# Gated delta-rule block: the decays take beta and the key norm as logarithms, and ScalarE takes over the roots

## The chip, the cores and the metric

The kernel runs on one core of one Trainium2 chip. The metric is the device time of one execution in microseconds. A NeuronCore has five instruction queues that run side by side and wait for one another through semaphores: TensorE (PE in the profile, with its weight loads as PEld), VectorE (DVE), ScalarE (ACT), GpSimd (POOL) and SyncE (SP), which here only issues DMAs. [...]

## What is computed

One transformer block in float32: an attention that supplies the hidden states, a gated delta rule over chunks of 64 tokens, and two feed-forward parts. The change touches only the delta rule. Cut to what matters:

```python
q = _l2norm(q); k = _l2norm(k)            # x * rsqrt(sum(x * x) + 1e-6)
beta = sigmoid(h @ W_b)
g = cumsum(-exp(A_log) * softplus(h @ W_a + dt_bias))     # in each chunk of 64
decay = tril(exp(g[:, None] - g[None, :]))
A = tril(-(k * beta) @ k.T * decay, -1)
T = inverse(I - A)
u = T @ (v * beta)
w = T @ (k * beta * exp(g))
...
core = core * rsqrt(mean(core * core) + 1e-6) * norm_w
core = core * silu(z)
return core @ W_out
```

There are 16 batches of 128 tokens (two chunks each), 16 key heads and 32 value heads of width 128.

## The kernel before

Attention comes first, in 32 blocks, and the delta rule starts while it is still running. The delta rule is cut into 64 **units**, each one key head (two value heads) with a group of four batches, that is 8 pairs of batch and value head. A loop over slots `n` runs the units as a software pipeline: in slot n the keys of unit n are made (`keys`), the key products of unit n-1 (`decays`), the values of unit n-7 (`values`), the outputs of unit n-8 (`outputs`), and unit n-10 is transposed and multiplied with its rows of `W_out` (`finish_unit`). In every four slots a batch of four units is inverted (`inverse`): 32 small triangular systems side by side, almost all on DVE, in a first and a second half that lie in two successive slots. `mergers` puts the 32x32 inverses together to 128x128 on PE.

Each step has a planned time between 0 and 24 in its slot, written by hand in the loop at the end. The steps of a slot are emitted in that order; the framework may then move an instruction a little, and each engine keeps the order that results. All PSUM tiles of this stage except `ps_out` come from one pool of six buffers, taken in turn: a tile waits for the one that was allocated six places earlier.

What the change touches:

- `logs` (lines 310 to 334): beta as 1 / (1 + exp(-x)), with an addition and a reciprocal on DVE (L323, L324), and the gates.
- `running` (336 to 347): cumulative sums of the gates by matmul. The rows go to DRAM (`sums`), the columns to SBUF (`off`).
- `load_sums` (428): for a **pair** of units, the sums of each broadcast over all partitions, 512 KB each, into a tile `aT` of 2048 columns.
- `fades` (436): for a pair, POOL subtracts `off` (L443) and masks (L444), and ACT takes one exponential of both (L448).
- `factors` (497), the last step of `keys`: POOL makes from the squared norms `nn` (L500, L502), by powers `kn` (L505: the norm and its inverse square), and the product `c` of beta and 1/norm² (L507).
- `weight` (519), the first step of `decays`: POOL multiplies the decays with `c` (L522). The products then multiply them with k kᵀ and k qᵀ on DVE (L534), which frees `ps_kq`. `diagonal` (537) writes the diagonal blocks to the tile that the inverse reads.
- `norm` (772), the last step of `outputs`: POOL adds the epsilon term (L775), takes the power -1/2 (L776) and multiplies z (L777).

Beside these, prediction and change speak of `conv` (459: one copy on ACT, three multiply-adds on DVE, L466), `row`, `times`, `merge8`, `products16` and `sums16` of the inverse (L568 to L628), `val_turn` (720: transposes of the values, `ps_vt`), `gate` (736: `ps_z` and its silu), `new_values` (748: `ps_y` and its copy to y) and `attend` (758: `ps_ot`).

ACT needs another set of function tables for Silu than for Exp and Ln; where the function changes, the build puts a table load (ACT_TABLE_LOAD) in front of it.

Of the kernel before, what the change touches and what calls it, by code (L numbers as in the profile page):

```python
# [15 lines left out]
P = 128  # L16
# [40 lines left out]
def tile_adaln_attn_ffn(  # L57
# [36 lines left out]
    powers = filled([P, 2, GS], 0.5, "powers")  # L94
    G.memset(powers[:, 1, :], -1.0)
    inv_root = filled([P, NP], -0.5, "inv_root")
# [38 lines left out]
    beta = keep.tile([P, NK, NB, 2], F32, name="beta")  # L135
# [14 lines left out]
    def attention():  # L150
# [144 lines left out]
        def output(g):  # L295
# [14 lines left out]
            def logs():  # L310
                if g > 1:
                    nc.sync.dma_start(out=h_dram[g], in_=hTs[g])
                ps = ps_b.tile([P, GS, 2 * NV], F32, name="ps_ba", tag="b")
                for j in range(GS):
                    for c in range(ND):
                        T.matmul(ps[:, j, :], lhsT=hTs[g][:, c, j * S : (j + 1) * S], rhs=wba[:, c, :],
                                 start=c == 0, stop=c == ND - 1)
                a = p1.tile([P, GS, NV], F32, name="a", tag="ga", bufs=1)
                e = p1.tile([P, GS, NV], F32, name="ea", tag="ge", bufs=1)

                A.activation(e, ps[:, :, 0:NV], AF.Exp, scale=-1.0)
                V.tensor_tensor(a, ps[:, :, NV:], dtb[:, None, :].to_broadcast([P, GS, NV]), ALU.add)
                V.tensor_scalar(e, e, 1.0, None, ALU.add)  # L323
                V.reciprocal(beta[:, :, g * GS : (g + 1) * GS, :].rearrange("p k b h -> p b k h"),  # L324
                             e.rearrange("p b (k h) -> p b k h", h=2))

                V.scalar_tensor_tensor(out=e, in0=a, scalar=-1.0, in1=a, op0=ALU.mult, op1=ALU.max)
                A.activation(e, e, AF.Exp, scale=-1.0)
                A.activation(e, e, AF.Ln, bias=one)
                V.scalar_tensor_tensor(out=a, in0=a, scalar=0.0, in1=e, op0=ALU.max, op1=ALU.add)  # L330
                gd = d["gd"] = p1.tile([P, NK, GS, 2], F32, name="gd", tag="gd", bufs=1)
                V.tensor_tensor(gd.rearrange("p k b h -> p b k h"), a.rearrange("p b (k h) -> p b k h", h=2),
                                nega.rearrange("p (k h) -> p k h", h=2)[:, None, :, :].to_broadcast([P, GS, NK, 2]),
                                ALU.mult)

            def running():
# [91 lines left out]
    def load_sums(n):  # L428

        t = sum_of[n] = pc.tile([P, 2, NP, S], F32, name="aT", tag="aT", bufs=5)  # L430
        for i in range(2):
            kh, g = units[n + i]
            nc.sync.dma_start(out=t[:, i].rearrange("p q t -> p (q t)"),
                              in_=sums[g][kh * NP : (kh + 1) * NP].rearrange("q t -> (q t)").partition_broadcast(P))

    def fades(n):

        def log(i):
            t = sum_of[n]
            kh, g = units[n + i]  # L440
            o = off[:, kh, g * GS : (g + 1) * GS].rearrange("p s h i -> p (s h) i")
            t4 = t[:, i].rearrange("p q (i c) -> p q i c", i=2)
            G.tensor_tensor(t4, t4, o[:, :, :, None].to_broadcast([P, NP, 2, C]), ALU.subtract)  # L443
            G.affine_select(out=t[:, i], in_=t[:, i], pattern=[[0, NP], [1, S]], compare_op=ALU.is_ge,  # L444
                            fill=-1e30, base=0, channel_multiplier=-1)

        def exp():
            A.activation(sum_of[n], sum_of[n], AF.Exp)  # L448

        return [lambda: log(0), lambda: log(1), exp]  # L450
# [20 lines left out]
    def keys(u):  # L471
# [10 lines left out]
        def silu(j):  # L482
            A.activation(d["kq"][:, :, j, :], d["kc", j], AF.Silu)  # L483
# [13 lines left out]
        def factors():  # L497
            tr = d["tr"][:, :, 0].rearrange("p (s j) -> p j s", j=2)
            nn = d["nn"] = pc.tile([P, 2, GS], F32, name="nn", tag="nn", bufs=10)
            G.tensor_scalar(nn[:, 0, :], tr[:, 0, :], 1e-6, None, ALU.add)  # L500

            G.tensor_scalar(nn[:, 1, :], tr[:, 1, :], 1e-6, P * P * 1e-6, ALU.add, ALU.mult)  # L502

            kn = d["kn"] = pc.tile([P, 2, GS], F32, name="kn", tag="kn", bufs=9)
            G.tensor_tensor(kn, nn[:, 0:1, :].to_broadcast([P, 2, GS]), powers, ALU.pow)  # L505
            d["c"] = pc.tile([P, GS, 2], F32, name="c", tag="c", bufs=2)
# [3 lines left out]
        return [lambda: qk(0), lambda: qk(1), lambda: silu(0), lambda: silu(1), square, norms, factors]  # L510

    def decays(u):
# [5 lines left out]

        def weight():
            n = index[u]  # L520
            dec = d["aT"] = sum_of[n - n % 2][:, n % 2]
            G.tensor_tensor(dec, dec, d["c"].rearrange("p s h -> p (s h)")[:, :, None].to_broadcast([P, NP, S]),  # L522
                            ALU.mult)
            d["bT"] = pc.tile([P, NP, S], F32, name="bT", tag="bT", bufs=7)
# [20 lines left out]
        return [weight, lambda: products(0), lambda: products(1), diagonal]  # L545
# [161 lines left out]
    def values(u):  # L707
# [9 lines left out]
        def silu(h):  # L717
            A.activation(d["vT", h], d["vT", h], AF.Silu)

        def val_turn(n):  # L720
# [4 lines left out]
            for j in range(2):  # L725
                s = 2 * n + j
                A.activation(d["v"][:, s, :, :], ps[:, j, :, :], AF.Copy, scale=d["kn"][:, 0, s : s + 1])
# [3 lines left out]
    def outputs(u):  # L731
# [4 lines left out]
        def gate(n):  # L736
# [8 lines left out]
            A.activation(d["z"][:, 4 * n : 4 * n + 4, :].rearrange("p q f -> p (q f)"),  # L745
                         ps.rearrange("p s f -> p (s f)"), AF.Silu)
# [25 lines left out]
        def norm():  # L772

            r = d["r"].rearrange("p (s h) -> p s h", h=2)
            G.tensor_tensor(r, r, d["nn"][:, 1, :][:, :, None].to_broadcast([P, GS, 2]), ALU.add)  # L775
            G.tensor_tensor(d["r"], d["r"], inv_root, ALU.pow)  # L776
# [3 lines left out]
                lambda: attend(0), lambda: attend(1), norm]  # L780
# [72 lines left out]
    for n in range(N + LAST):  # L853
# [14 lines left out]
        if n == 0:  # L868
            plan([lambda: load_sums(0)], [5])
# [278 lines left out]
```

## Time and profile before

| | us |
|---|---|
| three runs | 2427.54, 2430.64, 2430.76 (median 2430.64) |
| the profiled execution | 2431.28 |
| its span, from the first to the last instruction | 2429.6 |

| engine | busy us | share | instructions |
|---|---|---|---|
| PE | 2200.7 | 91% | 16248 |
| PEld | 1450.2 | 60% | 16248 |
| DVE | 1548.1 | 64% | 2102 |
| ACT | 1361.7 | 56% | 3008 |
| POOL | 1145.9 | 47% | 833 |

The profile comes from one execution with the hardware profiler. Busy shares are means over stages that have different limits: up to about 330 us attention and the first units run together, from there to about 1900 us the full pipeline, then it drains, and from about 2106 us the feed-forward parts run. The groups of instructions that the change removes or alters (count, busy us, mean ns of one):

| line, engine | what | count | busy | mean |
|---|---|---|---|---|
| L443 POOL | decays minus `off`, 128x1024 | 64 | 123.4 | 1929 |
| L444 POOL | causal mask, 128x1024 | 64 | 71.8 | 1124 |
| L500, L502 POOL | `nn`, 128x4 | 64 each | 15.6, 12.7 | 244, 198 |
| L505 POOL | `kn`, power, 128x8 | 64 | 106.9 | 1671 |
| L507 POOL | `c`, 128x8 | 64 | 51.8 | 810 |
| L522 POOL | weight, 128x1024 | 64 | 122.3 | 1911 |
| L775 POOL | r plus epsilon term, 128x8 | 64 | 30.8 | 481 |
| L776 POOL | power -1/2, 128x8 | 64 | 105.0 | 1640 |
| L777 POOL | z times r, 128x1024 | 64 | 132.2 | 2066 |
| L448 ACT | exponential of two units, 128x2048 | 32 | 61.2 | 1913 |
| all, ACT | table loads | 79 | 101.4 | 1283 |

Between two successive instructions of an engine there can be a wait; the trace names the instruction of another engine whose signal came last. A wait on PE costs time in the full pipeline, since PE is the engine with the least slack there; a wait on POOL as a rule costs none.

### The profile page before, as it was taken

How to read it: one execution, taken by the hardware profiler on the slowest of the kernel's cores; microseconds unless marked ns; L12 is line 12 of the kernel's file. 1: busy time of each engine (PE TensorE's matmuls, PEld its weight loads, DVE VectorE, ACT ScalarE, POOL GpSimd, SP SyncE). 2: the span in 40 equal slices, each digit the busy share in tenths (PEclk: the TensorE clock that was granted, in tenths of full speed). 3: DMA queues.
4: the chain of work that ended last, by engine and by line, in shares of the span. 5: the costliest groups of instructions: out<-in, count | busy, mean ns of one | idle time of the engine just before them, and what ended most of it. 6: DMA issues, size and time to landing. Idle time of an engine off the chain costs nothing. (4 is left out here: it accounts for less than half of the span.)

```text
span 2429.6 us, 41939 instructions
## 1 busy us (share of the span) xinstructions
PE 2200.7 (91%) x16248; PEld 1450.2 (60%) x16248; DVE 1548.1 (64%) x2102; ACT 1361.7 (56%) x3008; POOL 1145.9 (47%) x833
## 2 busy tenths in 40 slices
PE   7868759989999998989999998989999898999999
PEld 3433336766667666766666666766677686344445
DVE  4657878687776968687777868687876831311111
ACT  3566536766666666766666666766666574111110
POOL 4585535465555656465555656465556413700000
PEclk9889879999999999999999999999999999999999
DMA  1200022222222322322223222222322323000000
GB/s 56 91 17 15 24 56 76 70 66 71 68 66 77 104 72 64 75 68 68 68 80 86 82 73 64 77 66 68 85 69 80 89 52 123 26 0 20 9 0 18
DMA packets 289910, 148.37 MB, mean 61 GB/s; under 512 B 184241, under 2 KB 278193, under 8 KB 289713
## 3 DMA queue, kind: packets, MB, share of 16 engines
q1 hardware_dynamic: 287792, 141.44, 21.1%
q0 software_dynamic: 1344, 4.20, 0.5%
q8 instruction: 131, 2.15, 0.4%
q14 instruction: 67, 0.54, 0.1%
q10 hardware_dynamic: 576, 0.05, 0.0%
HBM read 119.13 MB, written 5.51 MB: 51 GB/s over the span
## 5 line engine op out<-in xcount | busy, mean ns | idle before, releaser
L466 DVE SCALAR_TENSOR_TENSOR cv<-ps_in,cw,cv 128x500 f32<-128x500 f32 (+2 forms) x768 | 540.2, 735 | 88.8 <-ACT cv L464 84.2
L455 PE MATMUL ps_in<-hT,w_v 128*128 128x512 f32 x512 | 281.5, 679 | 6.8 <-DVE z L770 4.6
L464 ACT ACTIVATE cv<-ps_in,cw 128x512 f32<-128x512 f32 x256 | 174.5, 682 | 182.7 <-PE ps_in L455 182.0
L770 DVE TENSOR_TENSOR z<-ps_ot,z 128x512 f32<-128x512 f32 x128 | 87.9, 687 | 289.9 <-ACT sq L768 289.9
L455 PE MATMUL ps_in<-hT,w_qk 128*128 128x512 f32 x512 | 251.3, 613 | 7.1 <-DVE z L770 6.2
L743 PE MATMUL ps_z<-w_gate,hT 128*128 128x256 f32 x1024 | 242.3, 379 | 1.7 <-DVE z L770 1.7
L800 PE MATMUL ps_out<-wo_head,zT 128*128 128x256 f32 x1024 | 238.8, 386 | 1.0 <-ACT zT L792 1.0
L500 POOL TENSOR_SCALAR nn<-turned 128x4 f32<-128x4 f32 x64 | 15.6, 244 | 419.4 <-DVE turned L495 316.8
L800 PEld LDWEIGHTS ps_out<-wo_head,zT 128*128 128x128 f32 x1024 | 189.0, 190 | 38.0 <-issue 10.7
L743 PEld LDWEIGHTS ps_z<-w_gate,hT 128*128 128x128 f32 x1024 | 189.4, 190 | 27.7 <-DVE z L770 2.6
L455 PEld LDWEIGHTS ps_in<-hT,w_v 128*128 128x128 f32 x512 | 104.6, 217 | 113.3 <-issue 105.2
L768 ACT ACTIVATE sq<-ps_ot 128x128 f32<-128x128 f32 x512 | 143.2, 280 | 31.6 <-PE ps_ot L762 23.0
L483 ACT ACTIVATE kq<-cv 128x512 f32<-128x512 f32 x128 | 80.1, 626 | 126.8 <-DVE cv L466 126.7
L756 ACT COPY y<-ps_y 128x512 f32<-128x512 f32 x128 | 75.0, 586 | 135.3 <-PE ps_y L755 130.6
L530 PEld LDWEIGHTS ps_kq<-kq 128*128 128x128 f32 x512 | 102.5, 203 | 73.4 <-issue 53.4
L455 PEld LDWEIGHTS ps_in<-hT,w_qk 128*128 128x128 f32 x512 | 94.2, 195 | 84.8 <-issue 67.0
L1055 POOL TENSOR_TENSOR o<-o,x_in 128x512 f32<-128x512 f32 x8 | 10.1, 1265 | 283.4 <-DVE o L1054 283.4
L777 POOL TENSOR_TENSOR z<-z,r 128x1024 f32<-128x1024 f32 x64 | 132.2, 2066 | 23.2 <-DVE z L770 20.4
L790 PE MATMUL ps_zt<-ident,z 128*128 128x128 f32 x512 | 88.9, 301 | 59.4 <-DVE aT L534 57.4
L530 PE MATMUL ps_kq<-kq 128*128 128x256 f32 x512 | 136.8, 391 | 0.0
L762 PE MATMUL ps_ot<-y,aT 128*128 128x128 f32 x1024 | 135.3, 275 | 0.0
L755 PEld LDWEIGHTS ps_y<-v,W 128*128 128x128 f32 x1024 | 123.3, 194 | 16.6 <-ACT W L701 10.8
(212 smaller groups left out, 5004.2 us busy)
## 6 DMA issues: line engine op xcount, KB each, us to landing
aT<-sums SPq DMA_DIRECT2D x64, 512.0 KB, 5.8
w_qk<-in_w_qkv_dram SPq DMA_DIRECT2D x128, 128.0 KB, 2.2
w_v<-in_w_qkv_dram SPq DMA_DIRECT2D x64, 256.0 KB, 2.7
w_gate<-in_w_z_dram SPq DMA_DIRECT2D x64, 256.0 KB, 2.7
wo_head<-in_w_out_dram SPq DMA_DIRECT2D x64, 256.0 KB, 2.7
diag<-bT SPq DMA_DIRECT2D x256, 32.0 KB, 2.0
W<-Uc SPq DMA_DIRECT2D x256, 32.0 KB, 2.0
T<-Tc SPq DMA_DIRECT2D x128, 32.0 KB, 1.9
```

What stands on the lines that cost most here:

```text
L455: T.matmul(ps, lhsT=w[:, c, blk, :], rhs=hTs[g][:, c, :], start=c == 0, stop=c == ND - 1)
L464: A.activation(cv, psv, AF.Copy, scale=cw[:, col, 3:4])
L466: V.scalar_tensor_tensor(out=cv[:, :, sh:], in0=psv[:, :, : S - sh], scalar=cw[:, col, 3 - sh : 4 - sh], in1=cv[:, :, sh:], op0=ALU.mult, ...
L530: T.matmul(ps[:, j, :, :], lhsT=d["kq"][:, s, 0, :], rhs=d["kq"][:, s, :, :], start=True, stop=True)
L743: T.matmul(ps[:, j, :], lhsT=hTs[g][:, c, t0 : t0 + S], rhs=w_gate[u][:, c, :], start=c == 0, stop=c == ND - 1)
L755: T.matmul(ps[:, j, :], lhsT=d["W"][:, p, :], rhs=v[:, p, :], start=True, stop=True)
L762: T.matmul(ps[:, j, :], lhsT=d["aT"][:, p, :], rhs=d["y"][:, p, :], start=True, stop=True)
L768: A.activation(sq, ps[:, j, :], AF.Square, accum_out=d["r"][:, p : p + 1])
L770: V.tensor_tensor(z, ps, z, ALU.mult)
L777: G.tensor_tensor(d["z"], d["z"], d["r"][:, :, None].to_broadcast([P, NP, S]), ALU.mult)
L790: T.transpose(ps[:, j, :], d["z"][:, 4 * n + j, :], ident)
L800: T.matmul(ps[:, j, :], lhsT=d["zT", n][:, 2 * j + h, :], rhs=w_o[u][:, h, :], start=kh == j == h == 0, stop=kh == NK - 1 and j == h == 1)
```

## The change

Beta and the key norm no longer enter as factors. The exponent of the decays gets their logarithms: `off` holds the cumulative gate plus softplus(-x), which is -log(beta), and a small tile `lk` = log(norm² + epsilon) is added for each unit before the subtraction. One exponential then gives decay, beta and 1/norm² together, so `weight` goes. `kn` = exp(lk / 2) serves the values, and the output norm is exp(-log(r) / 2). Both powers leave POOL. The load and five ACT instructions form one block per unit (`logarithms`): a load of the table set with Exp and Ln, the exponential of the unit before (128x1024), Ln and Exp of `r` of a unit nine slots back, Ln and Exp of the new key norms. By ordering edges the block stands behind every silu of the delta rule emitted before it and ahead of every later one (`silu_of`, `follow`). Decays are handled one unit at a time. Most planned times move; the `decays` products go from 4.5 and 9 to 18 and 21, the inverse's first half starts at 8, and the norm product comes one slot later.

```diff
-    powers = filled([P, 2, GS], 0.5, "powers")
-    G.memset(powers[:, 1, :], -1.0)
-    inv_root = filled([P, NP], -0.5, "inv_root")
+    small = filled([P, 1], 1e-6, "small")
...
-                A.activation(e, ps[:, :, 0:NV], AF.Exp, scale=-1.0)
+                sp = d["sp"] = p1.tile([P, GS, NV], F32, name="sp", tag="gs", bufs=1)
+                A.activation(sp, ps[:, :, 0:NV], AF.Exp, scale=-1.0)
...
-                V.tensor_scalar(e, e, 1.0, None, ALU.add)
-                V.reciprocal(beta[:, :, g * GS : (g + 1) * GS, :].rearrange("p k b h -> p b k h"),
-                             e.rearrange("p b (k h) -> p b k h", h=2))
+                A.activation(sp, sp, AF.Ln, bias=one)
...
-                    V.tensor_copy(off[:, :, g * GS : (g + 1) * GS, :, i].rearrange("p k b h -> p k (b h)"),
-                                  ps[:, 1 + i, :].rearrange("p (k q) -> p k q", k=NK))
+                    V.tensor_tensor(off[:, :, g * GS : (g + 1) * GS, :, i],
+                                    ps[:, 1 + i, :].rearrange("p (k b h) -> p k b h", k=NK, h=2),
+                                    d["sp"].rearrange("p b (k h) -> p k b h", h=2), ALU.add)
...
+        t = sum_of[n] = pc.tile([P, NP, S], F32, name="aT", tag="aT", bufs=9)
...
         def factors():
...
-            G.tensor_scalar(nn[:, 0, :], tr[:, 0, :], 1e-6, None, ALU.add)
-            G.tensor_tensor(kn, nn[:, 0:1, :].to_broadcast([P, 2, GS]), powers, ALU.pow)
-            G.tensor_tensor(d["c"], beta[:, kh, g * GS : (g + 1) * GS, :],
-                            kn[:, 1, :][:, :, None].to_broadcast([P, GS, 2]), ALU.mult)
+            G.tensor_scalar(nn, tr[:, 1, :], 1e-6, P * P * 1e-6, ALU.add, ALU.mult)
+        def fade():
+            t = d["aT"] = sum_of[index[u]]
+            o = pc.tile([P, GS, 2, 2], F32, name="o", tag="o")
+            G.tensor_tensor(o.rearrange("p s h i -> p s (h i)"),
+                            off[:, kh, g * GS : (g + 1) * GS].rearrange("p s h i -> p s (h i)"),
+                            d["lk"][:, :, None].to_broadcast([P, GS, 4]), ALU.add)
+            t4 = t.rearrange("p q (i c) -> p q i c", i=2)
+            G.tensor_tensor(t4, t4, o.rearrange("p s h i -> p (s h) i")[:, :, :, None].to_broadcast([P, NP, 2, C]),
+                            ALU.subtract)
+            G.affine_select(out=t, in_=t, pattern=[[0, NP], [1, S]], compare_op=ALU.is_ge,
+                            fill=-1e30, base=0, channel_multiplier=-1)
...
+    def logarithms(new, old, done):
...
+        block = [A.preload_act_table_set("natural_log_exp_and_others")]
+        if old:
+            block.append(A.activation(un[old]["aT"], un[old]["aT"], AF.Exp))
+        if done:
+            r = un[done]["r"]
+            block.append(A.activation(r, r, AF.Ln))
+            block.append(A.activation(r, r, AF.Exp, scale=-0.5))
+        if new:
+            block.append(A.activation(lk, un[new]["tr"][:, :, 0].rearrange("p (s j) -> p j s", j=2)[:, 0, :], AF.Ln, bias=small))
+            block.append(A.activation(kn, lk, AF.Exp, scale=0.5))
+        for ins in table["silus"]:
+            follow(block[0], ins)
+        for a, b in zip(block, block[1:]):
+            follow(b, a)
+        table["last"], table["silus"] = block[-1], []
...
+    def silu_of(dst, src):
+        ins = A.activation(dst, src, AF.Silu)
+        if table["last"]:
+            follow(ins, table["last"])
+        table["silus"].append(ins)
...
-        def weight():
-            G.tensor_tensor(dec, dec, d["c"].rearrange("p s h -> p (s h)")[:, :, None].to_broadcast([P, NP, S]),
-                            ALU.mult)
...
-            G.tensor_tensor(d["r"], d["r"], inv_root, ALU.pow)
...
-            plan(steps, [0, 0, 8, 14] if at(MERGE) else [14])
+            plan(steps, [2, 2, 7.5, 12] if at(MERGE) else [12])
+        if at(0):
+            plan(keys(at(0)), [1, 5, 5.5, 10.0, 12.0, 14, 15, 18])
+        if at(0) or at(1) or at(OUT + 1):
+            plan([lambda: logarithms(at(0), at(1), at(OUT + 1))], [15])
         if at(1):
-            plan(decays(at(1)), [0, 4.5, 9, 10])
-        if at(0):
-            plan(keys(at(0)), [2, 5, 6.0, 10, 12.0, 14, 19])
-        if n % 2 == 0 and n < N:
-            plan(fades(n), [8, 12, 19])
+            plan(decays(at(1))[:2], [18.0, 21])
+        if at(2):
+            plan(decays(at(2))[2:], [7])
         if at(MERGE):
-            plan(values(at(MERGE)), [5.5, 8.5, 9, 15.5, 18, 23])
+            plan(values(at(MERGE)), [5.5, 8.0, 13, 16.5, 19, 24])
         if at(OUT):
-            plan(outputs(at(OUT)), [13, 20, 16, 17, 19, 22, 23.5])
+            plan(outputs(at(OUT))[0], [13, 20, 16, 17, 19, 22, 23.5])
+        if at(OUT + 1):
+            plan([outputs(at(OUT + 1))[1]], [17.0])
         if at(LAST):
-            plan(finish_unit(at(LAST)), [0, 8, 14, 14])
+            plan(finish_unit(at(LAST)), [7, 7.5, 11.5, 18.5])
         if at(NU + 1) and (n - NU - 1) % NU == 0:
             first, second = inverse((n - NU - 1) // NU)
-            spread(first)
+            spread(first, 8)
         elif at(NU + 2) and (n - NU - 2) % NU == 0:
-            plan(second, [0, 1, 4, 6, 7, 13, 15, 17])
+            plan(second, [4.5, 5.5, 7, 9, 10, 14.5, 17, 23.5])
...
-        if n % 2 and n + 1 < N:
+        if 1 <= n < N - 1:
             load_sums(n + 1)
```

More of the change, by code (lines that the diff above doesn't have):

```diff
@@ L133, in tile_adaln_attn_ffn @@
     V.tensor_copy(rows_in, tokf)
-    beta = keep.tile([P, NK, NB, 2], F32, name="beta")
     off = keep.tile([P, NK, NB, 2, 2], F32, name="off")
@@ L428, in load_sums @@
     def load_sums(n):
[L430 to L450, printed above, removed]
+        kh, g = units[n]
+        t = sum_of[n] = pc.tile([P, NP, S], F32, name="aT", tag="aT", bufs=9)
+        nc.sync.dma_start(out=t.rearrange("p q t -> p (q t)"),
+                          in_=sums[g][kh * NP : (kh + 1) * NP].rearrange("q t -> (q t)").partition_broadcast(P))
     def mm_in(g, w, blk):
@@ L482, in silu @@
         def silu(j):
-            A.activation(d["kq"][:, :, j, :], d["kc", j], AF.Silu)
+            silu_of(d["kq"][:, :, j, :], d["kc", j])
         def square():
@@ L498, in factors @@
             tr = d["tr"][:, :, 0].rearrange("p (s j) -> p j s", j=2)
-            nn = d["nn"] = pc.tile([P, 2, GS], F32, name="nn", tag="nn", bufs=10)
-            G.tensor_scalar(nn[:, 0, :], tr[:, 0, :], 1e-6, None, ALU.add)
-            G.tensor_scalar(nn[:, 1, :], tr[:, 1, :], 1e-6, P * P * 1e-6, ALU.add, ALU.mult)
-            kn = d["kn"] = pc.tile([P, 2, GS], F32, name="kn", tag="kn", bufs=9)
-            G.tensor_tensor(kn, nn[:, 0:1, :].to_broadcast([P, 2, GS]), powers, ALU.pow)
-            d["c"] = pc.tile([P, GS, 2], F32, name="c", tag="c", bufs=2)
@@ L507, in factors @@
-            G.tensor_tensor(d["c"], beta[:, kh, g * GS : (g + 1) * GS, :],
-                            kn[:, 1, :][:, :, None].to_broadcast([P, GS, 2]), ALU.mult)
-        return [lambda: qk(0), lambda: qk(1), lambda: silu(0), lambda: silu(1), square, norms, factors]
+            nn = d["nn"] = pc.tile([P, GS], F32, name="nn", tag="nn", bufs=10)
+            G.tensor_scalar(nn, tr[:, 1, :], 1e-6, P * P * 1e-6, ALU.add, ALU.mult)
[10 more added lines that the diff above has]
+                            fill=-1e30, base=0, channel_multiplier=-1)
@@ new lines, in keys @@
+        return [lambda: qk(0), lambda: qk(1), lambda: silu(0), lambda: silu(1), square, norms, factors, fade]
+    def logarithms(new, old, done):
+        lk = kn = None
+        if new:
+            d = un[new]
+            lk = d["lk"] = pc.tile([P, GS], F32, name="lk", tag="lk")
+            kn = d["kn"] = pc.tile([P, GS], F32, name="kn", tag="kn", bufs=9)
+        if old:
+            d = un[old]
+            d["bT"] = pc.tile([P, NP, S], F32, name="bT", tag="bT", bufs=7)
+        block = [A.preload_act_table_set("natural_log_exp_and_others")]
+        if old:
+            block.append(A.activation(un[old]["aT"], un[old]["aT"], AF.Exp))
[3 more added lines that the diff above has]
+            block.append(A.activation(r, r, AF.Exp, scale=-0.5))
+        if new:
+            block.append(A.activation(lk, un[new]["tr"][:, :, 0].rearrange("p (s j) -> p j s", j=2)[:, 0, :], AF.Ln, bias=small))
[5 more added lines that the diff above has]
+        table["last"], table["silus"] = block[-1], []
@@ L512, in decays, with follow @@
+    table = {"last": None, "silus": []}
+    edge = mybir.DependencyInfo(mybir.DependencyClass.NoSync, mybir.DependencyReason.DATA)
+    def follow(ins, before):
+        tc.add_manual_dep(ins.ins, before.ins.name, edge, reason="table")
+    def silu_of(dst, src):
[3 more added lines that the diff above has]
+        table["silus"].append(ins)
     def decays(u):
@@ L517, in decays @@
         k = index[u] % NU
-        def weight():
-            n = index[u]
-            dec = d["aT"] = sum_of[n - n % 2][:, n % 2]
-            G.tensor_tensor(dec, dec, d["c"].rearrange("p s h -> p (s h)")[:, :, None].to_broadcast([P, NP, S]),
-                            ALU.mult)
-            d["bT"] = pc.tile([P, NP, S], F32, name="bT", tag="bT", bufs=7)
         def products(n):
@@ L543, in diagonal @@
                 nc.sync.dma_start(out=D_[b, NP * k : NP * (k + 1), :], in_=d["bT"][b, :, b])
-        return [weight, lambda: products(0), lambda: products(1), diagonal]
+        return [lambda: products(0), lambda: products(1), diagonal]
     def inverse(n):
@@ L717, in silu @@
         def silu(h):
-            A.activation(d["vT", h], d["vT", h], AF.Silu)
+            silu_of(d["vT", h], d["vT", h])
         def val_turn(n):
@@ L726, in val_turn @@
                 s = 2 * n + j
-                A.activation(d["v"][:, s, :, :], ps[:, j, :, :], AF.Copy, scale=d["kn"][:, 0, s : s + 1])
+                A.activation(d["v"][:, s, :, :], ps[:, j, :, :], AF.Copy, scale=d["kn"][:, s : s + 1])
         return [lambda: val(0), lambda: val(1), lambda: silu(0), lambda: silu(1), lambda: val_turn(0), lambda: val_turn(1)]
@@ L744, in gate @@
                              start=c == 0, stop=c == ND - 1)
-            A.activation(d["z"][:, 4 * n : 4 * n + 4, :].rearrange("p q f -> p (q f)"),
-                         ps.rearrange("p s f -> p (s f)"), AF.Silu)
+            silu_of(d["z"][:, 4 * n : 4 * n + 4, :].rearrange("p q f -> p (q f)"), ps.rearrange("p s f -> p (s f)"))
         def new_values(n):
@@ L770, in attend, with root @@
             V.tensor_tensor(z, ps, z, ALU.mult)
+        def root():
+            r = d["r"].rearrange("p (s h) -> p s h", h=2)
+            G.tensor_tensor(r, r, d["nn"][:, :, None].to_broadcast([P, GS, 2]), ALU.add)
         def norm():
-            r = d["r"].rearrange("p (s h) -> p s h", h=2)
-            G.tensor_tensor(r, r, d["nn"][:, 1, :][:, :, None].to_broadcast([P, GS, 2]), ALU.add)
-            G.tensor_tensor(d["r"], d["r"], inv_root, ALU.pow)
             G.tensor_tensor(d["z"], d["z"], d["r"][:, :, None].to_broadcast([P, NP, S]), ALU.mult)
         return [lambda: gate(0), lambda: gate(1), lambda: new_values(0), lambda: new_values(1),
-                lambda: attend(0), lambda: attend(1), norm]
+                lambda: attend(0), lambda: attend(1), root], norm
     def finish_unit(u):
@@ L868, in tile_adaln_attn_ffn @@
         if n == 0:
-            plan([lambda: load_sums(0)], [5])
+            plan([lambda: load_sums(0), lambda: load_sums(1)], [5, 5])
         if n == MERGE:
```

## The prediction

> **What bounds the kernel now.** I read the page's busy line first (PE 91%), then the slices, then four successive units in a table of windows, each cut where GpSimd starts the product z x r of a unit (L777). Columns: window, length, busy us with instruction counts for PE, weight loads, DVE, ACT and POOL, then granted clock, DMA share, GB/s.
>
> ```profile
> 658.84:683.05 24.21, 24.21 (x226) 18.06 (x225) 12.63 (x20) 16.15 (x42) 7.93 (x8) 1.00 0.32 80
> 683.05:712.01 28.96, 27.94 (x233) 19.24 (x231) 26.46 (x40) 21.34 (x46) 18.67 (x13) 1.00 0.25 69
> 712.01:743.39 31.38, 27.48 (x273) 19.46 (x272) 27.50 (x31) 17.02 (x42) 20.18 (x11) 0.95 0.30 83
> 743.39:768.11 24.72, 22.86 (x169) 17.50 (x170) 15.36 (x21) 19.23 (x42) 13.09 (x15) 0.86 0.20 49
> ```
>
> The first unit is TensorE back to back: 24.2 us with no gap, DVE half idle, POOL a third busy. That is the floor. Counted by the starts of ps_lo (L669), which mark a unit more evenly, the four take 24.2, 25.2, 29.4 and 30.4. The 25.2 holds the exponential of two units with its two table loads; 29.4 and 30.4 hold the batched inverse, most of it on DVE. So 12.4 us in four units is not floor, and about 11 of them belong to the inverse. Three places show how they arise (totals of the waits: us, times, longest; then lines in order of time: start, duration):
>
> ```profile
> PE ps_zt L790 <- DVE aT L534: 57.4, 26, 2.6
> DVE inv L628 <- POOL prod L578: 40.7, 11, 3.7
> ```
> ```profile
> 701.64 1.90 POOL L522 TENSOR_TENSOR aT<-aT,c 128x1024 f32<-128x1024 f32 x1
> ```
> ```profile
> 701.86 2.04 DVE L568 TENSOR_TENSOR prod<-lanes,inv 128x196 f32<-128x196 f32 x1
> ```
> ```profile
> 715.52 0.63 PE L790 MATMUL ps_zt<-ident,z 128*128 128x128 f32 x4 [2.58 <-DVE aT L534]
> 716.16 3.65 PE L455 MATMUL ps_in<-hT,w_v 128*128 128x512 f32 x4
> ```
>
> ps_zt takes the PSUM buffer that ps_kq held six allocations earlier; DVE frees it late, because inverse work stands ahead. And after the 2.58 us gap the same four matmuls take 3.65 instead of 1.88 us: the clock column drops too. A long gap costs itself and almost 2 us more.
>
> **POOL's part.** Gone per unit: both powers (L505 1671 ns, L776 1640), L507 (810), L500 (244) and the weight product L522 (1911), 6.28 us. Added: o = off + lk on 128x16. No such row; the nearest are L775 (481 mean) and, as ends, L507 at its shortest (0.20) and its mean (0.81). I take 0.48. Net -5.8 us a unit, 370 us of 1146. It ends no wait on a plain unit: POOL L500 waits 316.8 us in total for DVE's `turned`, so POOL is ahead and this is worth 0 there. It counts in two places, below.
>
> **ACT's part.** The build shows 161 table loads for 79. Per unit in the steady stage it was one (two for each pair, one exponential of 1913 ns for two units); it becomes two and an exponential of 1024, for which the attention's 1056 ns stands, plus four tiny Ln/Exp: nearest row L191, 230 ns on 128x32. Growth per unit: 1.28 + 0.1 + 0.92 = 2.3 us, 18.5 to 20.8 of ACT's busy time against a floor of 24.2. It fits as a sum; what matters is the queue. By the added edges every silu planned before stands ahead of the load, all later ones behind it. Queued behind are y (twice) and the silu of the second value half; the first attend (ps_ot) waits for y, ps_vt for that silu. I walk it from the end of ps_z: ACT 0.65 (silu of z), 1.28, 0.95, four times 0.2, two y at 0.5, 1.28, 0.62 = 6.6 us. PE in that time has ps_n 0.57, ps_y 1.8, ps_kq 0.87, half of ps_out 1.78, ps_vt 0.11, ps_ot 0.9, a quarter of ps_z 0.43 = 6.5 us. PE waits 0.1 to 0.4, call it 0.35 with signals. The changed PSUM order adds a possible wait: ps_in of the second value half takes the buffer of the q convolution, whose last DVE step stands behind one of v; 0 to 0.5, I take 0.25. So a plain pair pays 2 x 0.6 and no longer the 1.0 of the shared exponential: **+0.2**.
>
> Here the Trainium skill speaks against the change. Its page ScalarE: Activation LUTs, section What ACT_TABLE_LOAD costs, prices a switch at 2.66 us, 1.28 of load and 1.38 of drain. The row has 1283 ns, and at 751.92 the load is followed by the silu at 753.21: no drain to be seen. By the page two loads put 2.8 us more before that silu, a wait of 3.1 us in every unit, some 56 x 3 = 170 us; by the row 0.35. I use the row.
>
> **The inverse pair (59.8 us now).** At 701.86 DVE's 128x196 product takes 2.04 us (mean 1.99) where its row of 144 takes 0.42: it ends with POOL's L522. The Trainium skill's page SBUF — State Buffer, section SBUF: two separate sides, says that the two engines hold a port pair as an exclusive lock for whole instructions. With L522 gone 1.5 us go, but by the lock the POOL product Tc (2.85) still stops DVE's second merge product (3.12 against 1.04), and POOL's `prod` (5.5) can stop DVE's Tc. The wait of 40.7 us, 2.5 a batch, falls in part: the new times put convolutions between `gm` and the sum of `prod`. I take 1.3 of 2.5. Against both: the built order has nearly all of the first half, including the 3.81 us product, ahead of the next unit's first convolution: 23 to 25 us from `lanes` to there for 17 now. Slot one loses about 4 more, slot two 2 less: +1.8. Sum -1.5 - 1.3 + 1.8 = **-1.0**, with ends -4.5 (all wait gone, no pile-up) and +1.7 (nothing saved but the lock).
>
> **Head.** In the first 330 us attention shares POOL, and PE waits 40.9 us there for the softmax product L267. Eight units of keys lose 4.15 us each of POOL queue (no norm yet), 33 us; a third on the path: **-11**, ends 0 and -30. Table loads up to the last softmax go from 19 to 22; ACT is half idle there. Sigmoid: L323/L324 leave DVE, one Ln per group comes: 0.
>
> **At nothing.** Loads of sums are 64 either way (5.8 us to land), one unit a time, nine buffers for ten; they wait on SP for the last attend, and the diagonal DMAs stand behind them. Hidden by the half unit until `lanes`; if that cover is gone DVE waits up to 2 us a batch, within the pair's upper end. Norm product a slot later: z has three buffers, ps_zt follows ten steps on. The FFN tail from 2106 is unchanged: TensorE.
>
> **Sum.** 56 full units are 14 sets of four: 14 x (0.2 - 1.0) = -11; head -11. From the profiled execution's 2431.28 us (span 2429.6): **2409 us**. The median shown, 2430.64, is the same within 0.6.
>
> **Rivals.** (1) *ACT's block holds PE.* Place: ps_vt behind the second load. If the dependent Ln/Exp pairs or `turned` add 1 us, each unit gaps 1.2 instead of 0.35; decides once the block passes 7.5 us. 56 x 0.85 = +48, minus 22: **2457**. For it: only 0.1 us margin in my walk. Against: gaps of 0.7 (at ps_n) leave the clock at 1.00. (2) *The pile-up on DVE wins*: pair +1.7, plain +0.9: 14 x 2.6 - 11 = +25: **2456**. For: the order; against: 1.5 us of lock surely leave. (3) *DVE gets free*: pair -4.5, head -20: **2350**; for it the 40.7 us wait. (4) *Nothing*: POOL's work was hidden, ACT's is; **2431**.
>
> **Numbers.** Forecast 0.36, (1) 0.20, (2) 0.19, (3) 0.15, (4) 0.10. Faster by over 0.2% (4.9 us, what a measurement can tell) 0.51, within 0.10, slower 0.39. The range reaches to both slower cases with 15 us beyond, and most of the way to (3): 2365 to 2472. The likeliest case's own is 2385 to 2425.
>
> **What would show it.** Units by ps_lo near 25, 25, 33, 26 for the forecast; a wait of ps_vt for the silu below 0.5 us a unit; DVE's 128x196 row at 0.5 us; the L628 wait halved; ps_pt's wait in the head shorter. Wrong if ps_vt or ps_y gaps exceed 1 us in plain units, if a third long gap with a halved clock appears, or if a drain follows the loads.

## The result, and the profile after

The changed kernel takes 2408.32 us (median of 4 runs, 2407.95 to 2411.79) against 2430.2 us before: a ratio of 0.9915, 95% interval 0.9898 to 0.9932. The profiled executions span 2406.8 and 2429.6 us. The forecast was 2409, so the sum came out. Its terms did not: errors of different sign cancelled, which is luck, and the rest of this text is about the terms.

The busy line of the changed kernel shows work going from POOL to ACT (before: ACT 1361.7, POOL 1145.9, DVE 1548.1):

```profile
PE 2194.9 (91%) x16248; PEld 1432.5 (60%) x16248; DVE 1605.2 (67%) x2094; ACT 1482.6 (62%) x3382; POOL 755.0 (31%) x575
```

POOL lost 391 us, ACT gained 121. DVE has eight instructions fewer and is 57 us busier: the first sign that something stretches its instructions.

To see where the 22.8 us went I cut each span at two marks that every kernel has, the transposition of key norms (`turned`) of units 12 and 60. Up to unit 12 I call it the head, the 48 units (12 sets of four) between the steady stage, the rest the end (us):

| kernel | head | steady | end | span |
|---|---|---|---|---|
| before | 480.8 | 1310.6 | 638.1 | 2429.6 |
| after | 451.1 | 1309.7 | 645.9 | 2406.8 |
| difference | -29.7 | -0.9 | +7.7 | -22.8 |

All of the gain came from the head; a steady set takes 109.14 us for 109.22; the end gives some back. The four units of the windows, again cut where POOL starts z x r (L796), with the columns of the prediction's table:

```profile
647.67:672.22 24.55, 24.55 (x226) 17.83 (x225) 13.70 (x21) 19.90 (x50) 5.46 (x7) 1.00 0.31 79
672.22:700.62 28.40, 28.40 (x250) 21.11 (x249) 22.08 (x38) 23.70 (x59) 9.17 (x7) 1.00 0.32 79
700.62:728.55 27.93, 23.18 (x202) 15.64 (x201) 27.87 (x26) 16.32 (x39) 13.20 (x7) 0.88 0.18 54
728.55:752.09 23.54, 20.69 (x193) 14.31 (x192) 22.26 (x27) 16.25 (x42) 7.62 (x8) 1.00 0.36 85
```

This cut drifts, since z x r is late when POOL is; by the starts of ps_lo the four take 24.54, 24.55, 34.87 and 24.99, and most sets of the steady stage repeat these within 0.1. In the third row PE works 23.18 of 27.93 us, DVE all of it: the inverse still binds. Its place is new. The waits (total us, times, longest) of the changed kernel, then the lines of its timeline that make them:

```profile
PE ps_lo L688 <- DVE z L788: 41.6, 13, 3.7
PE ps_vt L743 <- ACT cv L533: 18.5, 19, 1.7
```
```profile
703.61 1.90 POOL L491 TENSOR_TENSOR aT<-aT,o 128x1024 f32<-128x1024 f32 x1
704.37 3.95 DVE L597 TENSOR_TENSOR prod<-inv,gm 128x512 f32<-128x512 f32 x2
708.24 0.68 DVE L788 TENSOR_TENSOR z<-ps_ot,z 128x512 f32<-128x512 f32 x1
708.98 1.06 PE L688 MATMUL ps_lo<-Tc,bT 32*32 32x32 f32 x30 [3.68 <-DVE z L788]
710.81 3.74 PE L435 MATMUL ps_in<-hT,w_qk 128*128 128x512 f32 x4 [0.78 <-PE ps_lo L688]
...
722.40 5.58 POOL L597 TENSOR_TENSOR prod<-inv,gm 128x2048 f32<-128x2048 f32 x1 [14.01 <-DVE gm L644]
...
724.76 5.00 DVE L597 TENSOR_TENSOR Tc<-inv,gm 128x1024 f32<-128x1024 f32 x1
```

The gap at ps_zt (57.4 us) is gone, and one at ps_lo (41.6) stands in its place: ps_lo needs a PSUM buffer that z must read first, and z stands behind two merge products on DVE. Those take 3.95 us together, as POOL's fade runs at the same time. Then four matmuls take 3.74 us for 1.88, at a granted clock of 0.52. At 724.76 a product of DVE waits out POOL's `prod`: 5.00 us, where it takes 1.90 when POOL stands still (run a_lock).

DVE's rows of the inverse by shape, before and after (busy us, mean ns | idle before, releaser). `prod<-lanes,inv` 128x512 are the first merge products, `prod<-inv,gm` 128x512 the second ones, two of each in a batch:

```profile
L578 DVE TENSOR_TENSOR prod<-lanes,inv 128x512 f32<-128x512 f32 x32 | 62.7, 1967 | 0.5
L578 DVE TENSOR_TENSOR Tc<-inv,gm 128x1024 f32<-128x1024 f32 x16 | 46.0, 2873 | 0.4
L628 DVE TENSOR_REDUCE inv<-prod 128x128 f32<-128x2048 f32 x16 | 36.5, 2282 | 40.7 <-POOL prod L578 40.7
L578 DVE TENSOR_TENSOR prod<-inv,gm 128x512 f32<-128x512 f32 x32 | 35.5, 1112 | 0.0
L568 DVE TENSOR_TENSOR prod<-lanes,inv 128x196 f32<-128x196 f32 x16 | 27.4, 1713 | 0.6
```
```profile
L597 DVE TENSOR_TENSOR Tc<-inv,gm 128x1024 f32<-128x1024 f32 x16 | 84.6, 5286 | 0.0
L597 DVE TENSOR_TENSOR prod<-lanes,inv 128x512 f32<-128x512 f32 x32 | 71.1, 2230 | 0.5
...
L597 DVE TENSOR_TENSOR prod<-inv,gm 128x512 f32<-128x512 f32 x32 | 54.4, 1730 | 0.1
...
L587 DVE TENSOR_TENSOR prod<-lanes,inv 128x196 f32<-128x196 f32 x16 | 8.5, 529 | 0.6
```

These rows hold all 16 batches. In the 12 batches of the steady stage alone, gone are 18.2 us of the 128x196 row (24.2 to 6.0) and the wait for `prod`, 33.5 us (3.7 in nine of the batches): 51.7 in all. New are 25.7 us of Tc product, 2.8 of first merge products and 16.9 of second ones: 45.4. The same instructions on the same data, stretched at other places. This is DVE's time; how much of each item reaches the kernel's time, the experiments have to show.

In the head, POOL is the engine to look at. The stretch from 120 to 180 us before, and after:

```profile
120.00:180.00 60.00, 40.88 (x170) 19.63 (x169) 30.68 (x47) 35.82 (x48) 54.26 (x39) 0.83 0.08 27
```
```profile
120.00:180.00 60.00, 56.17 (x254) 28.17 (x253) 43.91 (x69) 40.43 (x67) 31.85 (x20) 0.94 0.06 16
```

POOL goes from 54 to 32 us of 60, PE from 41 to 56. PE's waits for the softmax product (total us, times, longest), before and after:

```profile
PE ps_pt L274 <- POOL sc L267: 40.9, 12, 9.6
```
```profile
PE ps_pt L271 <- POOL sc L264: 15.7, 8, 6.1
```

What filled POOL before was not only powers and weights. Its timeline of the kernel before has this, among ten fades (L443, L444) in 46 us:

```profile
131.26 2.15 POOL L444 TENSOR_SCALAR_AFFINE_SELECT aT<-aT 128x1024 f32<-128x1024 f32 x2
133.38 3.75 POOL L443 TENSOR_TENSOR aT<-aT,off 128x1024 f32<-128x1024 f32 x2
137.09 1.89 POOL L267 TENSOR_TENSOR sc<-sc,sm 128x1024 f32<-128x1024 f32 x1
```

The fades before hang on nothing but a load and `off`, so those of ten units were pulled forward into the busiest part of attention, ahead of the softmax product L267 that PE waits for. After the change a fade needs `lk` of its unit and can't come early.

### The profile page after: what moved, and what is told of

Its sections match the earlier page's. It is cut to its first block, busy times and chain, and to the rows that moved or that the text cites. A ratio compares the mean times of both kernels' runs of the same rounds, so it can differ in the third digit from the quotient of the medians.

```text
span 2406.8 us, 41884 instructions
## 1 busy us (share of the span) xinstructions
PE 2194.9 (91%) x16248; PEld 1432.5 (60%) x16248; DVE 1605.2 (67%) x2094; ACT 1482.6 (62%) x3382; POOL 755.0 (31%) x575
## 5 line engine op out<-in xcount | busy, mean ns | idle before, releaser
L435 PE MATMUL ps_in<-hT,w_qk 128*128 128x512 f32 x512 | 274.1, 660 | 20.8 <-PE ps_lo L688 7.0
L444 ACT ACTIVATE cv<-ps_in,cw 128x512 f32<-128x512 f32 x256 | 174.7, 682 | 159.1 <-PE ps_in L435 154.1
L762 PE MATMUL ps_z<-w_gate,hT 128*128 128x256 f32 x1024 | 258.5, 387 | 12.3 <-DVE cv L446 12.3
L435 PE MATMUL ps_in<-hT,w_v 128*128 128x512 f32 x512 | 247.7, 607 | 5.0 <-DVE z L788 3.0
L819 PEld LDWEIGHTS ps_out<-wo_head,zT 128*128 128x128 f32 x1024 | 192.8, 191 | 53.5 <-issue 28.3
L762 PEld LDWEIGHTS ps_z<-w_gate,hT 128*128 128x128 f32 x1024 | 180.3, 190 | 35.8 <-DVE cv L446 14.5
L796 POOL TENSOR_TENSOR z<-z,r 128x1024 f32<-128x1024 f32 x64 | 148.9, 2327 | 139.6 <-ACT r L515 123.7
L597 POOL TENSOR_TENSOR prod<-inv,gm 128x2048 f32<-128x2048 f32 x16 | 89.0, 5564 | 230.7 <-DVE gm L644 230.7
L553 DVE TENSOR_TENSOR bT<-ps_kq,aT 128x512 f32<-128x512 f32 x128 | 87.5, 684 | 77.2 <-PE ps_kq L549 71.5
L780 PEld LDWEIGHTS ps_ot<-y,aT 128*128 128x128 f32 x1024 | 132.7, 196 | 10.0 <-ACT y L774 2.2
L597 DVE TENSOR_TENSOR prod<-lanes,inv 128x512 f32<-128x512 f32 (+1 forms) x48 | 131.2, 2738 | 0.5
L773 PE MATMUL ps_y<-v,W 128*128 128x128 f32 x1024 | 130.5, 281 | 0.0
```

The lines of the kernel that those rows point to most:

```text
L435: T.matmul(ps, lhsT=w[:, c, blk, :], rhs=hTs[g][:, c, :], start=c == 0, stop=c == ND - 1)
L444: A.activation(cv, psv, AF.Copy, scale=cw[:, col, 3:4])
L553: V.tensor_tensor(d[name][:, 4 * n : 4 * n + 4, :].rearrange("p (s h) t -> p s h t", h=2), ps[:, :, j : j + 1, :].to_broadcast([P, 2, 2, S ...
L597: engine.tensor_tensor(out_tile, lhs[:, :, None, :].to_broadcast([P, r, c, j]), rhs.rearrange("p j c -> p c j")[:, None, :, :].to_broadcas ...
L773: T.matmul(ps[:, j, :], lhsT=d["W"][:, p, :], rhs=v[:, p, :], start=True, stop=True)
L780: T.matmul(ps[:, j, :], lhsT=d["aT"][:, p, :], rhs=d["y"][:, p, :], start=True, stop=True)
```

## Experiments

Two questions: which of two causes made the head faster (A: the fades no longer bunch; B: POOL has less to do), and where the steady stage's expected 11 us went. The table gives every kernel in the three parts of its profiled execution, as difference to before in us; its time is the median, its ratio the one to the kernel before, run beside it.

| kernel | head | steady | end | time | ratio, interval |
|---|---|---|---|---|---|
| after | -29.7 | -0.9 | +7.7 | 2408.32 | 0.9915 [0.9898, 0.9932] |
| b_pin | +3.8 | +0.3 | -0.3 | 2439.15 | 1.0035 [1.0024, 1.0046] |
| b_less | -15.0 | -21.9 | -0.6 | 2400.53 | 0.9880 [0.9864, 0.9897] |
| b_both | -25.8 | -21.4 | -1.2 | 2385.44 | 0.9816 [0.9798, 0.9833] |
| a_free | -15.0 | -15.2 | +6.0 | 2406.67 | 0.9901 [0.9884, 0.9917] |
| a_block | -30.0 | +9.2 | +8.4 | 2422.61 | 0.9965 [0.9955, 0.9976] |
| a_edge | -28.9 | -26.3 | +6.3 | 2381.28 | 0.9805 [0.9784, 0.9826] |
| a_lock | -38.7 | +7.4 | +9.4 | 2409.94 | 0.9915 [0.9899, 0.9932] |
| a_both | -37.0 | +0.5 | +8.6 | 2407.02 | 0.9909 [0.9892, 0.9925] |
| a_vec | -28.3 | +0.3 | +8.7 | 2412.67 | 0.9928 [0.9911, 0.9944] |
| a_edge3 | -32.7 | -50.7 | +1.8 | 2348.46 | 0.9687 [0.9638, 0.9735] |
| a_swap3 | -30.2 | -0.1 | +8.5 | 2409.43 | 0.9906 [0.9889, 0.9922] |
| a_drain | -31.0 | -54.0 | +7.7 | 2355.17 | 0.9707 [0.9680, 0.9734] |

**b_pin: the kernel before, fades held back.**

```diff
+            ins = G.tensor_tensor(t4, t4, o[...], ALU.subtract)
+            if pin:
+                tc.add_manual_dep(ins.ins, pin[-1].ins.name, edge, reason="pin")
```

> The kernel before, with one thing added: each fade subtraction on GpSimd is ordered behind the last key factor emitted before it, so that the fades of later units can no longer be pulled ahead of the softmax steps in the head. No arithmetic and no GpSimd work goes. Theory A (the head's gain comes from the bunched fades being gone): 2400 to 2412 us, the time between the key norms of units 0 and 1 shorter by about 20 us. Theory B (the head's gain comes from GpSimd having less work: powers, weights and the weight product gone): 2426 to 2433, as before.

Neither theory. The key norm of unit 1 came 20 us earlier, as A has it, but by unit 9 the lead was gone, and the kernel ended slower than before. Unbunching alone only moves POOL's work about.

**b_less: the kernel before with POOL's work out, fades bunched.** The kernel leaves out the norms and the factor `c`; L500 and L507 stay.

```diff
-            G.tensor_tensor(kn, nn[:, 0:1, :].to_broadcast([P, 2, GS]), powers, ALU.pow)
+            G.tensor_tensor(kn, nn[:, 0:1, :].to_broadcast([P, 2, GS]), powers, ALU.mult)
...
-            G.tensor_tensor(dec, dec, d["c"]..., ALU.mult)
...
-            G.tensor_tensor(d["r"], d["r"], inv_root, ALU.pow)
+            G.tensor_tensor(d["r"], d["r"], inv_root, ALU.mult)
```

> The kernel before with GpSimd's work taken out and nothing else moved: both powers become multiplications (so the norms are not computed) and the weight product with c is left out; the fades stay bunched. Theory A: the head keeps its long stretch, key norms of units 0 and 1 as far apart as before within 6 us. Theory B: that distance falls by 15 us or more. In the steady stage the prediction's terms (1.5 us of port lock and 1.3 us of the wait for the product, per inverse pair, without the pile-up) would give 14 x 2.8 = 39 us: about 2390; if GpSimd's work is hidden there, 2425 to 2431.

Key norms of units 0 and 1 stay 45.8 us apart (48.3 before, 27.2 after), as A has it; the head still gains 15.0 by unit 12, so B has its half. The steady stage gains 1.83 a set, 21.9 in 12: of the prediction's 2.8 the lock came (24.2 to 6.0 us in the 128x196 row of the 12 batches, 1.5 each), while the wait for `prod` did not move (40.6 in all batches, 40.7 before). By the starts of ps_lo about half a us of a set lies outside the inverse, in the second plain unit (25.2 to 24.4 in most sets); why, I did not trace.

**b_both: both edits together** (the diffs of b_pin and b_less).

> The kernel before with GpSimd's work taken out (powers as multiplications, so no norms; weight product left out) and the fades ordered behind the key factors as well. So far, at the key norm of unit 8: work out alone -15.6 us against before, order alone -1.3, the changed kernel -30. If the head's gain is the two together (less work, and what is left not bunched): -24 to -32 at unit 8, time 2383 to 2393. If the other half comes from something else in the change: -12 to -18 at unit 8, time 2396 to 2404.

The head gives 25.8 of the change's 29.7 (-25.7 at unit 8): neither cause alone, but less work on POOL *and* no bunching. The two alone add to -11.2. Spreading POOL's queue won nothing while it held all its work, and 10.8 us once the work was out. The 3.9 us that are left I did not trace.

**a_free: the changed kernel with the fades set free.** The kernel leaves the key factor out of the decays.

```diff
-                            d["lk"][:, :, None].to_broadcast([P, GS, 4]), ALU.add)
+                            one[:, :, None].to_broadcast([P, GS, 4]), ALU.add)
```

> The changed kernel with the offset of a fade computed from a constant in place of the logarithm of the key norm (the key factor is left out of the decays), so that fades no longer wait for their unit's norm and can be pulled ahead again. GpSimd has the same instructions. Theory A: the fades bunch again and the head's gain goes: 2422 to 2436. Theory B: 2405 to 2412.

By its total B would be right; the parts say otherwise. Half of the head's gain goes (norms of units 0 and 1 again 45.4 apart), and the steady stage gains 14.3 against the changed kernel. The row that shows why is the second merge product, 1730 ns in the changed kernel:

```profile
L597 DVE TENSOR_TENSOR prod<-inv,gm 128x512 f32<-128x512 f32 x32 | 33.3, 1073 | 0.1
```

21 us of DVE gone with one dependency (16.9 of them in the steady stage): a fade that waits for `lk` falls on the merge product. The third unit takes 33.0 us for 34.9, the other three are the same. So the same dependency wins in the head and loses in the steady batches.

**a_block: ScalarE's block 1.0 us longer.**

```diff
-            block.append(A.activation(kn, lk, AF.Exp, scale=0.5))
+            for _ in range(6):
+                block.append(A.activation(kn, lk, AF.Exp, scale=0.5))
```

> The changed kernel with the last tiny exponential of ScalarE's block repeated five times more, about 1.0 us a unit longer ahead of the second table load. If the block stands at the edge of the path, as the prediction's walk has it (6.6 us against 6.5), PE waits about 1 us more at ps_vt in each of 56 units: 2440 to 2465. If the block is hidden by other work: 2405 to 2415.

Between the two: 10.1 us of steady stage for 48 x 1.03 us, a fifth of it on the path. ps_vt's wait rose from 18.5 us (19 times) to this:

```profile
PE ps_vt L744 <- ACT cv L534: 30.9, 60, 2.6
```

By the starts of ps_lo a plain unit takes 24.86 us for 24.54, 0.3 of the 1.03, and the inverse pair 59.81 for 59.86, none of it. The block does stand at an edge, but most of a longer one is covered.

**a_lock: POOL's products wait for DVE's; a_vec: DVE does them itself.**

```diff
-                    times(t[:, m], ...)
+                    st_["V"] = times(t[:, m], ...)
...
-                times(t, *args, G if part else V)
+                ins = times(t, *args, G if part else V)
+                if part:
+                    tc.add_manual_dep(ins.ins, st_["V"].ins.name, behind, reason="port")
+                elif second:
+                    st_["V"] = ins
```
```diff
-                times(t, *args, G if part else V)
+                times(t, *args)
```

> The changed kernel with each of GpSimd's two large inverse products made to wait for VectorE's neighbouring product (Tc behind the first merge products, prod behind the Tc product), so that the two engines no longer stand in each other's way. Same instructions. Theory A (what the change won from the lock it lost again to these two): VectorE's Tc product falls from 5.29 to about 1.95 us, the first merge products from 2.23 to about 1.1 us, 90 us of VectorE in 16 batches; the sum of prod then waits for GpSimd again by 1 to 3 us a batch; 2370 to 2398. Theory B (VectorE's stretched time is cover for waits that stand there anyway): 2400 to 2415.

> The changed kernel with GpSimd's two inverse products given to VectorE, which does 1.93 and 3.85 us more work a batch, 92 us in all, and is locked out 90 us less. If the lock makes the help of GpSimd worthless: 2395 to 2420, within 12 us of the changed kernel. If the help is worth its nominal 5.8 us a batch: 2460 to 2490.

The rows of a_lock:

```profile
L652 DVE TENSOR_REDUCE inv<-prod 128x128 f32<-128x2048 f32 x16 | 36.6, 2286 | 46.1 <-POOL prod L598 46.1
...
L598 DVE TENSOR_TENSOR Tc<-inv,gm 128x1024 f32<-128x1024 f32 x16 | 30.5, 1904 | 0.0
L649 DVE TENSOR_REDUCE gm<-Tc 128x128 f32<-128x1024 f32 x16 | 19.5, 1217 | 20.1 <-POOL Tc L598 20.1
```

The Tc product fell to 1.90 us as asked; the first merge products stayed at 2.21: at 688 us they run beside POOL's z x r and its fade. 66 us of waits for POOL came back, and the steady stage is 8.3 us longer than the changed kernel's: locked or waiting, DVE is late by POOL's product. (The head is 9.1 us shorter, which is why the total is the same; I did not trace it.) In a_vec, without POOL's help, the steady stage is the same within 1.3 us. In this place POOL's help was worth nothing.

**a_edge: another order in DVE's queue; a_both: the same with a_lock's edit.**

```diff
-            V.tensor_tensor(z, ps, z, ALU.mult)
+            table["z"] = V.tensor_tensor(z, ps, z, ALU.mult)
...
+                    if table.get("z"):
+                        follow(ins, table["z"])
```

> The changed kernel with one order edge: VectorE's second merge product (two of 128x512) stands behind the four PSUM products of its unit (z, bT, aT, z) in place of ahead of them. Same instructions. In the changed kernel ps_lo waits 41.6 us in all for that z, and the merge product meets GpSimd's fade (1730 ns a piece; 1073 where the fade came earlier). Theory A (the order in VectorE's queue sets PE's gaps): ps_lo's wait under 15 us, merge product near 1.1 us, 2360 to 2392. Theory B (VectorE is full for the whole inverse pair, 57.5 us without a hole, so order moves gaps only): the gap comes back in the second slot, 2395 to 2412.

> The two edits of the order edge and of the waits of GpSimd's products together. If they act on different gaps, their gains add: 2335 to 2380. If both only shift the same full queue of VectorE: no better than the better of the two, within 5 us.

For a_edge theory A holds: 25 us of steady stage from the order of six instructions a batch. The fade now runs beside steps that read PSUM, the merge product is back at 1143 ns, and ps_lo waits 4.6 us for z, not 41.6. The steady stages of the changed kernel, of a_edge and of a_edge3 (below), with the columns of the windows above, show where the time went:

```profile
451.15:1760.87 1309.72, 1221.47 (x10753) 874.19 (x10753) 1041.36 (x1326) 959.27 (x2305) 423.50 (x336) 0.97 0.29 74
```
```profile
451.91:1736.29 1284.38, 1210.87 (x10753) 869.73 (x10753) 1028.59 (x1326) 961.63 (x2305) 417.40 (x336) 0.99 0.29 76
```
```profile
448.10:1708.00 1259.90, 1202.03 (x10753) 867.42 (x10753) 1003.88 (x1327) 960.20 (x2305) 415.59 (x336) 0.99 0.29 77
```

In a_edge PE idles 14.7 us less (73.5 for 88.2), and the same number of matmuls takes 10.6 us less at a granted clock of 0.99 for 0.97. So two fifths of what the order edge won are faster matmuls, the rest is less waiting. What is left is the first line, and a new late one, the second:

```profile
L597 DVE TENSOR_TENSOR Tc<-inv,gm 128x1024 f32<-128x1024 f32 x16 | 91.7, 5733 | 0.0
```
```profile
PE ps_kq L549 <- DVE cv L446: 35.0, 14, 4.4
```

a_both lost a_edge's gain again: `gm` waited 23.8 and `inv` 46.0 us for POOL, and z stands behind them.

**a_edge3: two more edges.**

```diff
+                if second and not part:
+                    follow(ins, table["cv"])
...
+                if part:
+                    follow(ins, st_["sum"])
```

> The order edge of before (merge product behind the four PSUM products) and two more: VectorE's Tc product stands behind the last convolution step of its slot, the sum of prod behind the sum of Tc. Same instructions. With one edge PE still waits 35.0 us in 14 places at ps_kq, for the convolution step that stands behind the locked Tc product (5.73 us); GpSimd's prod runs in that time anyway, so Tc should only lose the time it was locked out. If so: Tc product near 4 us, the wait at ps_kq under 8, and 14 x 2 to 14 x 3 us gained: 2338 to 2358. If VectorE's full queue only moves the gap on: 2374 to 2385.

The Tc product moves behind the last convolution step of its slot, so that DVE spends POOL's 5.6 us on PSUM steps; the sum of `prod` moves behind the sum of Tc. Which of the two edges won how much, no run separates.

```profile
L597 DVE TENSOR_TENSOR Tc<-inv,gm 128x1024 f32<-128x1024 f32 x16 | 58.3, 3646 | 0.0
```
```profile
PE ps_lo L695 <- DVE Tc L659: 32.5, 15, 3.4
```

ps_kq's wait is gone from the head of the list. It is the fastest kernel here, 3.1% under the one before, with a set in 104.99 us. Of the 49.8 us that its steady stage is shorter than the changed kernel's, PE's idle time gives 30.4 and shorter matmuls 19.4. ps_lo's wait for the transposed Tc, which comes from the inverse's own length, is now the longest.

**a_swap3: the smaller product to POOL; a_drain: the last norms a slot earlier.**

```diff
-                ins = times(t, *args, G if part else V)
-                if second and not part:
+                ins = times(t, *args, G if part != second else V)
+                if second and part:
```
```diff
-            plan([outputs(at(OUT + 1))[1]], [17.0])
+            plan([outputs(done)[1]], [17.0])
+        if at(OUT) and n >= N:
+            plan([lambda: logarithms(None, None, at(OUT)), outputs(at(OUT))[1]], [23.7, 23.8])
```

> As the kernel with three edges, and the second pair of inverse products changed over: GpSimd gets the one of 1024, VectorE the one of 2048. The lock is then held 2.8 us by GpSimd in place of 5.6, VectorE has 1.9 us more of its own. If the lock decides: VectorE's product near 4 us, no worse than with three edges, 5 to 20 us better. If VectorE's sum of work decides: 14 x 1 to 2 us worse than with three edges.

> As the kernel with three edges, and from the last unit of keys on the root and the product of a unit's norm follow its attend steps in the same slot, as before the change, in place of a slot later. Between the units of 48 to 51 and the end, the changed kernel gave back about 5 us of its lead. If that comes from the norm a slot late: 2340 to 2345. If it is the shape of the drain itself (ScalarE's loads and the waits there are few, 3.6 us more than before in all): 2346 to 2352, which also measures the kernel with three edges once more.

a_swap3 lost all of a_edge3's gain in the steady stage. Its product on DVE took 4988 ns (3968 in a_vec, without POOL's); the sum of POOL's product (19.0 us of wait) came ahead of convolution steps in DVE's queue, and ps_lo waited 60.4 us for Tc. Since the order moved too, the run does not separate the lock from DVE's sum of work. a_drain gained nothing (end 645.8 us, 639.9 in a_edge3; the ratios' intervals overlap): the norm a slot late is not what the end gives back. Its cause stays open.

## Why the prediction was right in sum and wrong in its terms

**Steady stage, forecast -11, measured -0.9 in 12 of the 14 sets.** The step that failed is the inverse pair, "Sum -1.5 - 1.3 + 1.8 = -1.0". The pair took 59.86 us, the same as before (29.37 + 30.49). Both gains came: 1.5 us a batch from the 128x196 row, as forecast, and 2.8 from the wait for `prod`, more than forecast. The pile-up came too: from `lanes` to the next unit's first convolution step DVE takes 26.7 us for 17.0, where 23 to 25 were forecast; the third unit rose by 5.5 us and the fourth fell by 5.5, where 4 and 2 were forecast. What the sum lacks is the lock in its new spots, 3.8 us of DVE a batch. The prediction named the rule (by the lock POOL's Tc "still stops DVE's second merge product", the second of the first pair; `prod` "can stop DVE's Tc"), priced only the spot that goes, and put these at nothing. It also did not look where the new fade would fall. That spot counts in full: in a_free, where the second merge products run unlocked, `lanes` to convolution is 24.8 us, and the pair takes 58.0. The stretch of the Tc product, 2.1 a batch, gave nothing back in a_lock and a_vec. The rule of the Trainium skill, SBUF — State Buffer, section SBUF: two separate sides (an exclusive lock for whole instructions), agrees with 1.90 us alone against 5.29 beside `prod`.

The wait for `prod` was read as a matter of order alone. But POOL is locked out too: the prediction took 5.5 us for its `prod`, and in the kernel before it takes 7.3 in nine of the 12 steady batches, the very nine in which DVE waited 3.7 us. After the change it takes 5.6 in all of them. Two ends of the pair do not follow from its terms: -1.5 - 2.5 is -4.0, not -4.5, and "nothing saved but the lock" is -1.5 + 1.8 = +0.3, not +1.7. With +0.3, rival (2) would stand near 2437, not at 2456.

**Plain pair, forecast +0.2, measured -0.3.** Walked from 49.4 to 49.6, it takes 49.1. The exponential's 1.0 us went as said. No gap of PE over 0.1 us stands in the two plain units of the windows, so the 0.35 at ps_vt and the 0.25 at ps_in are not seen there. What a unit still pays, 0.3 us over 24.2, shows as longer matmuls at a clock of 1.00 (ps_z 4.05 us for 3.78, ps_vt 1.42 for 1.20). The profile models the ends of matmuls, so a short wait could hide in them; the cause stays open. In a_block 0.3 of one us more block reaches a plain unit. That ends rival (1), which put 0.85 of one us on the path of every unit; the walk, which let nothing change places on PE, was too strict.

**Table loads.** The prediction weighed the row, 1283 ns, against the Trainium skill, ScalarE: Activation LUTs, section What ACT_TABLE_LOAD costs (2.66 us a switch, drain included). The row was right. All 96 loads of the changed kernel's steady stage start within 0.02 us of the end of the instruction ahead, and the next one starts within 0.02 us of theirs. In a plain unit:

```profile
672.84 1.28 ACT L533 ACT_TABLE_LOAD   x1
674.13 0.63 ACT L533 ACTIVATE cv<-cv 128x512 f32<-128x512 f32 x1
```

No drain shows, and the 170 us that the prediction estimated from the page's figure did not come.

**Head, forecast -11, measured -29.7.** "A third on the path" of 33 us of POOL queue is near what b_less measured (-15.0). Missing was the second half, that the fades can no longer be pulled ahead: the diff shows the new dependency on `lk`, and the trace of before showed the bunch at 112 to 158 us. It was not read for order.

**Drain and tail, forecast 0, measured +7.7**, of which 3.4 after the last key norm. The cause stays open. The three terms were off by about 10, 19 and 8 us, and that these cancelled is luck.

**Signs.** ps_pt's wait fell from 40.9 to 15.7, the 128x196 row to 0.53, the wait of L628 for `prod` went wholly; the third unit was long and the fourth short, as named (24.5, 24.5, 34.9, 25.0 for 25, 25, 33, 26). Of the signs of being wrong none came: no gap over 1 us in plain units, no drain, and in most sets one stretch at half clock, where the kernel before has two.

## What to carry to other kernels

When a change takes work from an engine that shares a port, count the locks that appear at the new places as carefully as the one that goes: here 51.7 us of lock and waiting left DVE in twelve batches and 45.4 of lock came. Then look at what stands behind the locked instruction in its queue; three order edges, without a single instruction less, were worth 60 us, more than twice the change, and part of that was TensorE's clock, which falls after some gaps. And a dependency is also a brake on the scheduler: one that seems to cost may keep work out of a queue where it does harm.

## What the runs showed of the hardware

- The lock stopped DVE's products of two operands in SBUF and, in the places below, nothing else that ran beside POOL. In the changed kernel, with POOL's `prod` from 722.40 to 727.98, convolution steps, which read PSUM, took 0.70 to 0.72 us (their mean is 0.74), and the Tc product 5.00. In a_lock a sum over one SBUF operand took 1.20 us beside `prod` (1.21 is its mean) and a transposition 1.96 beside a fade. POOL pays too: its Tc took about 3.8 us in nine of the 12 steady batches of the changed kernel, 2.8 to 2.9 in a_lock, and its `prod` 7.3 in most batches of the kernel before, 5.6 after.
- A PE gap of 3.68 us was followed by four matmuls at half speed (3.74 for 1.88 us, granted clock 0.52). The length of one gap does not decide it. In a_edge the same gap of 0.81 us stands ahead of ps_z eleven times between 480 and 1800 us: the first eight matmuls after it took their usual 1.99 us eight times, and 3.30 to 3.53 three times. The ten gaps of 2.7 us ahead of ps_kq were followed by the usual 1.57 us for eight matmuls five times, by 2.29 to 2.93 five times. So "a long gap costs itself and almost 2 us more" holds for some gaps only.
- Ln or Exp on 128x4 and 128x8 took 0.19 to 0.33 us each on ACT; the powers on 128x8 that they replace took POOL 1.64 and 1.67 on average, and a multiplication in their place (b_less) 0.20.
